# Multi-level linear attention stage: GpSimd in program order, expert-row gathers by quarters, narrow state sums, turned keys, and three small moves in the scan stage

## The chip, the cores and the metric

One core of one Trainium2 chip runs the whole program. The metric is the device time of one execution in microseconds, the median of three runs. The trace is of one further, profiled execution, which has a time of its own.

## What is computed

A stack of four layers, each an attention-like half and a feed-forward half behind an adaptive layer norm, works on 32 sequences of 256 tokens with 128 features. The change touches two halves. The first is the selective scan of layer 0:

```python
delta = softplus(delta @ dt_W.T + dt_b)             # and softplus of the two convolutions
h = exp(delta * A) * h + delta * u * B               # 16 states for each of 128 features, along 256 tokens
y = sum_n(h * C) + u * D                             # two branches, then x = x + ga * (y*z + h)
```

The second, which gives the change its name, is the attention of layer 1. For each of 16 heads of width 8 it adds a causal linear attention and four more of the same kind, whose keys and values are causal block means over 2, 4, 8 and 16 tokens (`L` levels), and mixes the sum with a local softmax attention over 64 tokens:

```python
phi = lambda t: elu(t) + 1
for each of two chunks of 128 tokens:
    out  = phi(q) @ s_kv + causal(phi(q) @ phi(k).T) @ v     # s_kv: sum of phi(k).T @ v of the chunk before
    norm = the same with v = 1
glob = sum over 5 sets of (out / norm) * weight
```

The input of this half is the output of the expert layer before it, which lies in DRAM, two rows (one for each chosen expert) for each token. They are gathered by row number and added with their weights.

## The kernel before

**Layout.** `x` is kept in 16 tiles `x[b]` of 128 features by 512 tokens (two sequences). The stages of `run` (L2741) follow one another; the scan is `scan_layer` (L637), the multi-level attention is `hale` (L1544).

**Who sets the order.** Work is written as an agenda: `put(t, f)` hangs a function on a step `t`, and the agenda is run through in order of `t`. That is the program order. Only instructions that go through `keep_in_program_order` are held to it: TensorE's always (L386, L390), ScalarE's where `strict_act` is set, and VectorE's where `nc.vector.on` is set (class `InOrder`, L288). All the others are placed by the toolchain's planner, which sends the earliest written of those that it believes ready to an idle engine. In the scan, TensorE and ScalarE are in program order, VectorE and GpSimd are planned. In `hale`, TensorE alone is in program order.

**The scan.** For each tile there are eight steps `p` (two branches of four groups of four states); a tile begins every 16 agenda steps, an even and an odd one for each `p`. `scan_even` (L828) has TensorE fill all four banks of `dB` (16 matmuls), VectorE run four scans `hs` (L847), and then issues `scan_weigh(p-2, 1)`, `scan_turned(p-1, 0)` and `scan_decay(p+1, 0)`; `scan_odd` (L852) issues the other halves. `scan_turned` (L865) transposes half of `hs` into `hT` (one buffer) and ScalarE copies it to `hsT`; `scan_weigh` (L877) sums `hsT` with `Cd` into `y`; `scan_decay` is two exponentials on ScalarE. Beside them each tile has its preparation: four times `soft_start` (L734; `Abs` on ScalarE and `max(x+b, 0)` on VectorE, both from the one PSUM buffer `tp`) and `soft_end` (L741; Exp, Ln, and an addition on GpSimd), `scan_rows` (L765), `scan_b`, `scan_c`; and its end, `scan_end` (L899): VectorE adds `y`, GpSimd multiplies by `z` and adds `h`, and `residual` (L525) on VectorE writes `x[b]`. Here k stands for p modulo 8; the end of a tile falls on the odd step of k = 1 of the next.

**The multi-level attention.** `hale_slots` (L1589) gives each of 32 sequences `q` sixteen steps from `T = 16q`. Steps T to T+5 are the local attention (`hale_window`, with the maxima `hale_max` of the next sequence beside it), steps T+6 to T+15 the five linear attentions in two chunks each: `hale_scores` (L1873) fills two `S` tiles (two buffers in all), one is masked by VectorE (L1888), the other is copied by ScalarE (L1890) and masked by GpSimd (L1891, `affine_select`), and one step later `hale_weighted` (L1895) multiplies both with the values. The rest is hung between: 

- `gather_rows` (L1234) at T-48 for even q (T = 32b): eight indirect DMAs from GpSimd's queue into `got` (one buffer), and `gather_add` (L1249) at T-38: `gather_sum` on VectorE (L1261, L1262), four transposes, `residual`.
- `hale_values` (L1807): values of one half, and for half 0 the keys of set 0 in rows (`w.vvk`), through `phi` (L1655: Exp and Relu on ScalarE, one VectorE instruction) into `kt[:, 0]`.
- `hale_level_values(a, 0, pair)` (L1818): keys and values of two levels for half 0, keys through `phi` into `kt`; `hale_level_values(a, 1, None)`: values of all four for half 1.
- `hale_features` (L1835) and `hale_level_keys` (L1850): keys in columns for the scores, through `phi` into `f`; and GpSimd's `qG` (L1843).
- `hale_states` (L1861): `kt` times the values of half 0, 256 columns for each of five sets, masked by VectorE into `kvs`.
- `hale_divide` (L1927) transposes, divides and lets GpSimd add into `glob` (L1957); `hale_gate` (L1959) mixes and writes the residual.

All of these share three PSUM buffers `tp`. Within a step, first the `main` matmuls are issued, then their ScalarE, VectorE and GpSimd parts, then `side`, then `last`:

```python
            if s == 0:
                if self.gather:
                    put(side, T - 48, lambda b=b: self.gather_rows(b))
                    put(side, T - 38, lambda b=b: self.gather_add(0, b))
...
            put(side, T - 3, lambda a=a: self.hale_level_values(a, 0, 0))
            put(side, T - 2, lambda a=a: self.hale_level_keys(a, 0))
            put(side, T - 2, lambda a=a: self.hale_states(a, (0, 1)))
            put(side, T + 0, lambda a=a: self.hale_level_keys(a, 1))
            put(side, T + 1, lambda a=a: self.hale_level_values(a, 0, 1))
            put(side, T + 2, lambda a=a: self.hale_level_values(a, 1, None))
            put(side, T + 3, lambda a=a: self.hale_states(a, (2, 3)))
            put(side, T + 4, lambda a=a: self.hale_states(a, (4,)))
```

Of the kernel before, what the change touches and what calls it, by code (L numbers as in the profile page):

```python
# [30 lines left out]
P = 128  # L31
# [144 lines left out]
def packs(d):  # L176
# [40 lines left out]
    k.add("WoT", g["Wo"].T)  # L217
    k.add("Wk", g["Wk"])
    k.add("Wv", g["Wv"])
    k.add("vvk", np.concatenate([g["Wv"].T, g["Wvl"].T, by_heads(g["Wk"].T, DENSE)], 1))  # L220
# [67 lines left out]
class InOrder:  # L288
# [4 lines left out]

    def __getattr__(self, name):
        op = getattr(self.engine, name)
        if not self.on:
            return op
        return lambda *args, **kw: self.tc.keep_in_program_order(op(*args, **kw))  # L298


class Engines:
    def __init__(self, tc):
        self.nc = tc.nc
        self.vector = InOrder(tc, tc.nc.vector)

    def __getattr__(self, name):
        return getattr(self.nc, name)
# [2 lines left out]
class Program:  # L310
# [326 lines left out]
    def scan_layer(self, w):  # L637
# [7 lines left out]
        with ExitStack() as ctx:  # L645
# [28 lines left out]
            for b in range(NB):  # L674
                a = s[b] = {"b": b}
                T = 16 * b
                put(T, self.clear_regions)

                for o, n, src in ((T - 40, 1, lambda a: self.x[a["b"]]), (T - 32, 2, lambda a: a["h"])):
                    put(o, lambda a, n=n, src=src: a.update({("st", n): self.norm_rows(src(a), self.nc.gpsimd)}), a)  # L680
                    put(o + 1, lambda a, n=n: self.scan_roots(a, n), a)
                    put(o + 3, lambda a, n=n: self.norm_scale(a["st", n][0], *a["r", n]), a)
                put(T - 36, self.scan_norm_out, a)
                put(T - 28, self.scan_norm_out2, s, a)
                put(T - 23, self.scan_proj, s, a)
# [12 lines left out]
                put(T + 19, self.scan_end, s, a)  # L698
            for t in sorted(agenda):
                for f, args in agenda[t]:  # L700
                    f(*args)
# [126 lines left out]
    def scan_even(self, s, p):  # L828

        nc = self.nc  # L830
        if 0 <= p < 8 * NB:
# [13 lines left out]
            for n in range(4):  # L845
                decay = s["decay"][(4 * p + n) % 10].rearrange("p s t -> p (s t)")
                nc.vector.tensor_tensor_scan(hs[:, :, n], decay, dB[:, :, n], 0.0, ALU.mult, ALU.add)  # L847
# [51 lines left out]
    def scan_end(self, s, a):  # L899
        nc = self.nc  # L900
        py = self.ps("tp", (P, 4, P))
        for i in range(4):
            self.tr(py[:, i, :], a["yT"][:, i, :])
        y = self.wk("y")
        cut = dict(i=4, r=32)
        nc.vector.tensor_tensor(
            y.rearrange("p (q i r) -> p q i r", **cut),
            a["uu"].rearrange("p (q i r) -> p q i r", **cut),
            py.rearrange("p i (q r) -> p q i r", q=4),
            ALU.add,  # L910
        )
        nc.gpsimd.tensor_tensor(y, y, a["z"], ALU.mult)
        nc.gpsimd.tensor_tensor(y, y, a["h"], ALU.add)
        self.residual(0, 0, a["b"], y)


    def clear_regions(self):
# [313 lines left out]
            j, n = a["j"], m["BLK"]  # L1231
            self.nc.sync.dma_start(m["eo"][j * n : (j + 1) * n, :].rearrange("(t p) f -> p t f", p=P), eo)

    def gather_rows(self, b):  # L1234

        got = self.wk("got", (P, 4, 2, P))
        for t in range(4):
            for k in (0, 1):
                self.nc.gpsimd.indirect_dma_start(
                    out=got[:, t, k, :],  # L1240
                    out_offset=None,
                    in_=self.gather["eo"][:, :],
                    in_offset=bass.IndirectOffsetOnAxis(ap=self.back[:, k, 4 * b + t : 4 * b + t + 1], axis=0),
                    bounds_check=self.gather["rows"] - 1,
                    oob_is_err=False,
                )
        self.gather[b] = got

    def gather_add(self, layer, b):  # L1249
        self.gather_sum(b, range(4))  # L1250
# [293 lines left out]
    def hale(self, w):  # L1544
        nc, c = self.nc, self.c
        BF = mybir.dt.bfloat16
        with ExitStack() as ctx:
# [38 lines left out]
            self.strict = False  # L1586
            self.gather = None

    def hale_slots(self, w):  # L1589
# [9 lines left out]
        for q in range(2 * NB):  # L1599
# [26 lines left out]
            put(side, T - 6, lambda a=a: self.hale_values(w, a, 0))  # L1626
            put(side, T - 5, lambda a=a: self.hale_values(w, a, 1))
            put(side, T - 4, lambda a=a: self.hale_features(w, a))
            put(side, T - 3, lambda a=a: self.hale_level_values(a, 0, 0))
            put(side, T - 2, lambda a=a: self.hale_level_keys(a, 0))  # L1630
            put(side, T - 2, lambda a=a: self.hale_states(a, (0, 1)))
            put(side, T + 0, lambda a=a: self.hale_level_keys(a, 1))
            put(side, T + 1, lambda a=a: self.hale_level_values(a, 0, 1))
            put(side, T + 2, lambda a=a: self.hale_level_values(a, 1, None))
            put(side, T + 3, lambda a=a: self.hale_states(a, (2, 3)))
            put(side, T + 4, lambda a=a: self.hale_states(a, (4,)))
            for n in range(5):
                for i in (0, 1):
                    t = T + 6 + 2 * n + i
# [8 lines left out]
        for t in range(min(side), max(side) + 1):  # L1648
            then = [work() for work in main.get(t, [])]
            for work in then:  # L1650
                work()
# [154 lines left out]

    def hale_values(self, w, a, t):  # L1807

        n = 3 if t == 0 else 2
        pv = self.ps("tp", (P, n, P))  # L1810
        self.mm(pv, a["h"][:, t * P : (t + 1) * P], w.vvk[:, 0 : n * P])
        self.nc.vector.tensor_copy(
            self.vzb[t][:, :, :, 0:8], pv[:, 0:2, :].rearrange("p n (h d) -> p n h d", d=8)
        )
        if t == 0:
            self.phi(self.kt[:, 0, :], pv[:, 2, :])

    def hale_level_values(self, a, t, pair):  # L1818

        if t == 0:  # L1820
            pv = self.ps("tp", (P, 2, 2, P))
            for l in (0, 1):
                lvl = 2 * pair + l
                self.mm(pv[:, l], a["hm"][:, lvl, 0:P], self.wl[:, lvl])
            lv = slice(2 * pair, 2 * pair + 2)
            src = pv[:, :, 1, :]
            self.phi(self.kt[:, 1 + 2 * pair : 3 + 2 * pair, :], pv[:, :, 0, :])
        else:
            src = self.ps("tp", (P, 4, P))
            for lvl in range(4):  # L1830
                self.mm(src[:, lvl, :], a["hm"][:, lvl, P:], self.wl[:, lvl, 1, :])
            lv = slice(0, 4)
        self.nc.vector.tensor_copy(self.vzl[t][:, lv, :, 0:8], src.rearrange("p l (h d) -> p l h d", d=8))

    def hale_features(self, w, a):  # L1835

# [23 lines left out]

    def hale_states(self, a, ns):  # L1861

        pk = self.ps("tp", (P, len(ns), SEQ))
        for m, n in enumerate(ns):
            self.mm(pk[:, m, :], self.kt[:, n, :], self.set_values(n, 0)[:, :, 0:16])
        self.nc.vector.tensor_tensor(
            self.kvs[:, ns[0] : ns[-1] + 1, :],
            pk,
            self.c.same.unsqueeze(1).to_broadcast([P, len(ns), SEQ]),
            ALU.mult,  # L1870
        )

# [928 lines left out]
```

## Time and profile before

| What | Value |
|---|---|
| median of three runs | 6856.3 us (6840.84 to 6861.61) |
| the profiled execution | 6756.19 us, its span 6754.3 us, mean granted clock of TensorE 0.934 |
| scan stage, first to last scan instruction | 125.0 us to 1144.3 us |
| `hale`, first TensorE instruction to the next stage | 1717.9 us to about 3840 us |
| one tile in the scan (eight steps), in the middle | 64.8 us |
| two sequences (one tile) in `hale`, in the middle | 130.4 us |

A line of the groups reads: source line, engine, operation, what is written from what, shapes, count, busy time and mean of one, then the idle time of the engine just before them and what ended it. A line of the waits reads: who waited, on whom, total time, how often, the longest. A line of the timeline reads: start, duration, engine, line, operation, and in brackets the idle time before it and what ended that. PEld is TensorE's weight load; POOL is GpSimd, DVE VectorE, ACT ScalarE. The trace counts a float32 matmul as two instructions.

### The profile page before, as it was taken

To read this page: it belongs to the slowest core of one execution; us is meant where nothing else is said; L and a number is where in the kernel's file an instruction comes from. 1 tells how busy PE (TensorE), PEld (TensorE's weight loads), DVE (VectorE), ACT (ScalarE), POOL (GpSimd) and SP (SyncE) were. 2 spreads that over 40 slices of the span, in tenths; PEclk is the share of its full clock that TensorE was granted. 3 is DMA by queue.
4 is the path that set the end of the run, shared out by engine and by line. 5 is a ranking of instruction groups with operands and counts; after the bars stand their busy time and mean duration, and the time that the engine had idled before them with its cause. 6 is when DMAs were issued, how large, how long until landed. Compare 5 with 4: busy or idle time off the path is not lost. (4 is left out here: it accounts for less than half of the span.)

```text
span 6754.3 us, 132930 instructions
## 1 busy us (share of the span) xinstructions
PE 5907.4 (87%) x54209; PEld 3313.6 (49%) x54209; DVE 4350.0 (64%) x10025; ACT 3557.5 (53%) x5227; POOL 2660.5 (39%) x2881
## 2 busy tenths in 40 slices
PE   5777776899899999999999887999889998999987
PEld 3555555457555555555566444454422222444444
DVE  3666766621466666666666572888677774777779
ACT  5888885233344444444445442444478886544532
POOL 3555553566444444444444362444244543000000
PEclk7999998899899999999999877999999998989988
DMA  1101101135100000000000101111133442000010
GB/s 60 41 28 41 41 29 36 41 109 134 28 7 5 5 5 8 5 5 8 5 2 2 45 4 38 25 27 28 31 84 90 92 91 48 15 18 18 18 33 30
DMA packets 175447, 232.27 MB, mean 34 GB/s; under 512 B 46519, under 2 KB 95919, under 8 KB 174450
## 3 DMA queue, kind: packets, MB, share of 16 engines
q1 hardware_dynamic: 120656, 124.47, 7.3%
q0 software_dynamic: 26992, 56.62, 3.6%
q10 hardware_dynamic: 27186, 42.67, 1.7%
q8 instruction: 426, 6.98, 0.4%
q14 instruction: 187, 1.53, 0.1%
HBM read 88.28 MB, written 74.97 MB: 24 GB/s over the span
## 5 line engine op out<-in xcount | busy, mean ns | idle before, releaser
L1416 ACT ACTIVATE E<-S 128x1024 f32<-128x1024 f32 x448 | 459.0, 1025 | 592.8 <-PE S L386 579.4
L847 DVE TENSOR_TENSOR_SCAN hs<-decay,dB 128x512 f32<-128x512 f32 x512 | 583.1, 1203 | 196.9 <-PE dB L386 114.7
L298 DVE TENSOR_REDUCE mt<-S 128x4 f32<-128x1024 f32 (+1 forms) x512 | 550.2, 1088 | 224.5 <-PE S L386 223.8
L386 PE MATMUL S<-qa,kx 32*128 32x256 f32 x4096 | 556.2, 392 | 59.6 <-DVE mt L298 59.1
L393 ACT ACTIVATE hid<-S,bigw 128x1024 f32<-128x1024 f32 x512 | 537.6, 1112 | 124.2 <-PE S L386 124.0
L1888 DVE TENSOR_TENSOR E<-S,cst 128x1024 f32<-128x1024 f32 x320 | 391.2, 1223 | 301.1 <-PE S L386 300.5
L1891 POOL TENSOR_SCALAR_AFFINE_SELECT E<-E 128x1024 f32<-128x1024 f32 x320 | 350.2, 1094 | 594.6 <-ACT E L1890 594.2
L386 PE MATMUL S<-kx,q 32*128 32x512 f32 (+1 forms) x2048 | 540.4, 623 | 17.1 <-ACT kx L1534 16.1
L1890 ACT COPY E<-S 128x1024 f32<-128x1024 f32 x320 | 323.7, 1012 | 315.1 <-PE S L386 315.1
L2440 POOL TENSOR_TENSOR acc<-acc,ye 128x512 f32<-128x512 f32 x256 | 344.7, 1347 | 360.4 <-DVE ye L298 318.1
L386 PEld LDWEIGHTS S<-qa,kx 32*128 32x128 f32 x4096 | 350.8, 195 | 174.6 <-DVE mt L298 137.1
L1713 DVE TENSOR_REDUCE mt<-S 128x4 f32<-128x512 f32 (+1 forms) x256 | 205.2, 823 | 294.0 <-PE S L386 293.8
L386 PE MATMUL S<-qG,f 32*128 32x512 f32 x2560 | 382.3, 657 | 7.5 <-DVE E L1888 6.4
L386 PE MATMUL S<-hm,bigw 32*128 32x512 f32 x2048 | 338.7, 654 | 25.2 <-ACT hid L393 25.2
L393 ACT ACTIVATE hsT<-hT 128x1024 f32<-128x1024 f32 x256 | 260.4, 1017 | 179.7 <-PE hT L390 179.4
L390 PE MATMUL hT<-cst,hs 128*128 128x128 f32 x2048 | 285.9, 283 | 75.4 <-ACT hsT L393 73.5
L393 ACT ACTIVATE decay<-dl,A 128x510 f32<-128x510 f32 x512 | 339.2, 714 | 0.0
L386 PE MATMUL po<-E,vzl 128*32 128x128 f32 x8192 | 284.1, 279 | 50.1 <-POOL E L1891 50.1
L1760 ACT ACTIVATE E<-S 128x768 f32<-128x768 f32 (+1 forms) x192 | 169.1, 881 | 280.7 <-PE S L386 279.9
L390 PEld LDWEIGHTS hT<-cst,hs 128*128 128x128 f32 x2048 | 225.1, 143 | 169.6 <-ACT hsT L393 139.7
L386 PE MATMUL po<-E,vz 128*32 128x256 f32 x4096 | 300.2, 379 | 7.2 <-POOL E L1420 6.9
L386 PE MATMUL po<-hid,bigw 128*32 128x512 f32 x2048 | 277.2, 613 | 30.4 <-DVE ye L298 30.4
(520 smaller groups left out, 13307.8 us busy)
## 6 DMA issues: line engine op xcount, KB each, us to landing
gb<-gT SPq DMA_DIRECT2D x256, 256.0 KB
regions<-zeros ACTq DMA_DIRECT2D x16, 2048.0 KB
rx<-far SPq DMA_DIRECT2D x64, 256.0 KB
expert_rows<-eo SPq DMA_DIRECT2D x39, 256.0 KB
out<-out SPq DMA_DIRECT2D x16, 256.0 KB
xTd<-xT SPq DMA_DIRECT2D x15, 256.0 KB
xT<-xTd SPq DMA_DIRECT2D x15, 256.0 KB
bigw<-in_s SPq DMA_DIRECT2D x10, 256.0 KB
```

What stands on the lines that cost most here:

```text
L298: return lambda *args, **kw: self.tc.keep_in_program_order(op(*args, **kw))
L386: return self.tc.keep_in_program_order(self.nc.tensor.matmul(out, lhsT, rhs, start=start, stop=stop, **kw))
L390: return self.tc.keep_in_program_order(self.nc.tensor.transpose(out, in_, self.c.ident[:k, :k]))
L393: ins = self.nc.scalar.activation(*args, **kw)
L847: nc.vector.tensor_tensor_scan(hs[:, :, n], decay, dB[:, :, n], 0.0, ALU.mult, ALU.add)
L1416: nc.scalar.activation(e, src, AF.Exp, scale=scale)
L1713: nc.vector.tensor_reduce(m.rearrange("p (g j) -> p g j", j=2), pm[:, :, x] if i == 0 else pm[:, :, :, 0:192], AX.X, ALU.max, negate=True,)
L1760: nc.scalar.activation(e, src, AF.Exp, scale=1.0 / math.sqrt(8))
L1888: nc.vector.tensor_tensor(e, src, self.c.caus.unsqueeze(1).to_broadcast([P, 8, P]), ALU.mult)
L1890: nc.scalar.copy(e, src)
L1891: nc.gpsimd.affine_select(e, e, [[0, 8], [1, P]], ALU.is_ge, 0.0, base=0, channel_multiplier=-1)
L2440: nc.gpsimd.tensor_tensor(a["acc"], a["acc"], ye, ALU.add)
```

## The change

In the scan: `soft_start` no longer uses ScalarE's `Abs`; VectorE makes `m = src - 2 r` from `r = max(src + bias, 0)`, and `soft_end` takes `exp(m + bias)`. The residual of a tile is written two steps later in the agenda. `scan_even` issues `scan_weigh` after `scan_turned` and `scan_decay`.

In `hale`: GpSimd is held to program order (its DMAs are not, but each gather now reads its row numbers from `own`, a small copy that is). A tile's gather is split into four quarters of two DMAs, at T-62, T-58, T-54 and T-50, the sums at T-52 to T-40, the transposes and the residual stay at T-38. The row-wise keys of half 0 are no longer multiplied out: `hale_turn_keys` transposes the column-wise ones. The state sums take nine columns of each head in place of sixteen, and `kvs` is zeroed once.

```diff
 class InOrder:
-        if not self.on:
+        if not self.on or "dma" in name:
             return op
 class Engines:
         self.vector = InOrder(tc, tc.nc.vector)
+        self.gpsimd = InOrder(tc, tc.nc.gpsimd)
...
                 put(T + 19, self.scan_end, s, a)
+                put(T + 21, lambda a: self.residual(0, 0, a["b"], a["y"]), a)
     def soft_start(self, src, bias):
         m, r = self.wk("sp_m"), self.wk("sp_r")
-        self.act(m, src, AF.Abs, bias=bias)
         self.nc.vector.tensor_scalar(r, src, bias, 0.0, ALU.add, ALU.max)
-        return m, r
-    def soft_end(self, out, m, r):
-        self.act(m, m, AF.Exp, scale=-1.0)
+        self.nc.vector.scalar_tensor_tensor(m, r, -2.0, src, ALU.mult, ALU.add)
+        return m, r, bias
+    def soft_end(self, out, m, r, bias):
+        self.act(m, m, AF.Exp, bias=bias)
     def scan_even(self, s, p):
-        self.scan_weigh(s, p - 2, 1)
         self.scan_turned(s, p - 1, 0)
         self.scan_decay(s, p + 1, 0)
+        self.scan_weigh(s, p - 2, 1)
     def scan_end(self, s, a):
-        self.residual(0, 0, a["b"], y)
-    def gather_rows(self, b):
+    def gather_rows(self, b, quarters=range(4)):
+        got = self.gather[b]
+        for t in quarters:
+            at = [self.back[:, k, 4 * b + t : 4 * b + t + 1] for k in (0, 1)]
+            if nc.gpsimd.on:
+                own = self.wk("own", (P, 2), I32)
+                nc.gpsimd.tensor_copy(own, self.back[:, :, 4 * b + t])
+                at = own[:, 0:1], own[:, 1:2]
             for k in (0, 1):
...
     def hale(self, w):
+            nc.gpsimd.memset(self.kvs, 0.0)
-            self.strict = True
+            self.strict = nc.gpsimd.on = True
     def hale_slots(self, w):
-                    put(side, T - 48, lambda b=b: self.gather_rows(b))
-                    put(side, T - 38, lambda b=b: self.gather_add(0, b))
+                    for t in range(4):
+                        put(last, T - 62 + 4 * t, lambda b=b, t=t: self.gather_rows(b, (t,)))
+                        put(side, T - 52 + 4 * t, lambda b=b, t=t: self.gather_sum(b, (t,)))
+                    put(side, T - 38, lambda b=b: self.gather_end(0, b))
-            put(side, T - 3, lambda a=a: self.hale_level_values(a, 0, 0))
-            put(side, T - 2, lambda a=a: self.hale_level_keys(a, 0))
-            put(side, T - 2, lambda a=a: self.hale_states(a, (0, 1)))
-            put(side, T + 0, lambda a=a: self.hale_level_keys(a, 1))
-            put(side, T + 1, lambda a=a: self.hale_level_values(a, 0, 1))
-            put(side, T + 2, lambda a=a: self.hale_level_values(a, 1, None))
-            put(side, T + 3, lambda a=a: self.hale_states(a, (2, 3)))
-            put(side, T + 4, lambda a=a: self.hale_states(a, (4,)))
+            put(side, T - 3, lambda a=a: self.hale_level_keys(a, 0))
+            put(side, T - 2, lambda a=a: self.hale_level_keys(a, 1))
+            put(side, T + 0, lambda a=a: self.hale_level_values(a, 0))
+            put(side, T + 1, lambda a=a: self.hale_turn_keys(a, (0, 1, 2)))
+            put(side, T + 2, lambda a=a: self.hale_level_values(a, 1))
+            put(side, T + 3, lambda a=a: self.hale_turn_keys(a, (3, 4)))
+            put(side, T + 4, lambda a=a: self.hale_states(a, (0, 1, 2)))
+            put(side, T + 5, lambda a=a: self.hale_states(a, (3, 4)))
     def hale_values(self, w, a, t):
-        n = 3 if t == 0 else 2
-        pv = self.ps("tp", (P, n, P))
-        self.mm(pv, a["h"][:, t * P : (t + 1) * P], w.vvk[:, 0 : n * P])
+        pv = self.ps("tp", (P, 2, P))
+        self.mm(pv, a["h"][:, t * P : (t + 1) * P], w.vv)
...
-        if t == 0:
-            self.phi(self.kt[:, 0, :], pv[:, 2, :])
+    def hale_level_values(self, a, t):
+        pv = self.ps("tp", (P, 4, P))
+        for lvl in range(4):
+            self.mm(pv[:, lvl, :], a["hm"][:, lvl, t * P : (t + 1) * P], self.wl[:, lvl, 1, :])
+        self.nc.vector.tensor_copy(self.vzl[t][:, :, :, 0:8], pv.rearrange("p l (h d) -> p l h d", d=8))
+    def hale_turn_keys(self, a, ns):
+        pk = self.ps("tp", (P, len(ns), P))
+        for m, n in enumerate(ns):
+            self.tr(pk[:, m, :], a["f"][:, 1 + n, 0:P])
+        self.nc.scalar.copy(self.kt[:, ns[0] : ns[-1] + 1, :], pk)
     def hale_states(self, a, ns):
-        pk = self.ps("tp", (P, len(ns), SEQ))
+        pk = self.ps("tp", (P, len(ns), 16, 9))
         for m, n in enumerate(ns):
-            self.mm(pk[:, m, :], self.kt[:, n, :], self.set_values(n, 0)[:, :, 0:16])
+            self.mm(pk[:, m], self.kt[:, n, :], self.set_values(n, 0)[:, :, 0:9])
+        same = self.c.same.rearrange("p (h d) -> p h d", d=16)[:, :, 0:9]
         self.nc.vector.tensor_tensor(
-            self.kvs[:, ns[0] : ns[-1] + 1, :],
+            self.kvs[:, ns[0] : ns[-1] + 1, :].rearrange("p n (h d) -> p n h d", d=16)[:, :, :, 0:9],
...
```

More of the change, by code (lines that the diff above doesn't have):

```diff
@@ L219, in packs @@
     k.add("Wv", g["Wv"])
-    k.add("vvk", np.concatenate([g["Wv"].T, g["Wvl"].T, by_heads(g["Wk"].T, DENSE)], 1))
+    k.add("vv", np.concatenate([g["Wv"].T, g["Wvl"].T], 1))
     k.add("haar_Wk", np.stack([by_heads(diag_blocks(g["haar_Wk"][lvl].T, 16), DENSE) for lvl in range(4)], 1))
@@ L903, in scan_end @@
             self.tr(py[:, i, :], a["yT"][:, i, :])
-        y = self.wk("y")
+        y = a["y"] = self.wk("y")
         cut = dict(i=4, r=32)
@@ L1232, in block_out @@
             self.nc.sync.dma_start(m["eo"][j * n : (j + 1) * n, :].rearrange("(t p) f -> p t f", p=P), eo)
-    def gather_rows(self, b):
-        got = self.wk("got", (P, 4, 2, P))
-        for t in range(4):
+    def gather_rows(self, b, quarters=range(4)):
+        nc = self.nc
+        if 0 in quarters:
+            self.gather[b] = self.wk("got", (P, 4, 2, P))
+        got = self.gather[b]
[5 more added lines that the diff above has]
+                at = own[:, 0:1], own[:, 1:2]
             for k in (0, 1):
-                self.nc.gpsimd.indirect_dma_start(
+                nc.gpsimd.indirect_dma_start(
                     out=got[:, t, k, :],
@@ L1242, in gather_rows @@
                     in_=self.gather["eo"][:, :],
-                    in_offset=bass.IndirectOffsetOnAxis(ap=self.back[:, k, 4 * b + t : 4 * b + t + 1], axis=0),
+                    in_offset=bass.IndirectOffsetOnAxis(ap=at[k], axis=0),
                     bounds_check=self.gather["rows"] - 1,
@@ L1246, in gather_rows @@
                 )
-        self.gather[b] = got
     def gather_add(self, layer, b):
@@ L1582, in hale @@
             nc.vector.tensor_scalar(sw, sw, mx, None, ALU.mult)
-            self.strict = True
+            self.strict = nc.gpsimd.on = True
             self.use_ln_exp()
             self.hale_slots(w)
-            self.strict = False
+            self.strict = nc.gpsimd.on = False
             self.gather = None
@@ L1647, in hale_slots @@
                 put(side, T + 20 + 2 * n, lambda a=a, n=n: self.hale_gate(w, a, n))
-        for t in range(min(side), max(side) + 1):
+        for t in range(min([*side, *last]), max(side) + 1):
             then = [work() for work in main.get(t, [])]
@@ L1807, in hale_values @@
     def hale_values(self, w, a, t):
-        n = 3 if t == 0 else 2
-        pv = self.ps("tp", (P, n, P))
-        self.mm(pv, a["h"][:, t * P : (t + 1) * P], w.vvk[:, 0 : n * P])
-        self.nc.vector.tensor_copy(
-            self.vzb[t][:, :, :, 0:8], pv[:, 0:2, :].rearrange("p n (h d) -> p n h d", d=8)
-        )
-        if t == 0:
-            self.phi(self.kt[:, 0, :], pv[:, 2, :])
[L1818 to L1833, printed above, removed]
+        pv = self.ps("tp", (P, 2, P))
+        self.mm(pv, a["h"][:, t * P : (t + 1) * P], w.vv)
+        self.nc.vector.tensor_copy(self.vzb[t][:, :, :, 0:8], pv.rearrange("p n (h d) -> p n h d", d=8))
+    def hale_level_values(self, a, t):
[8 more added lines that the diff above has]
+        self.nc.scalar.copy(self.kt[:, ns[0] : ns[-1] + 1, :], pk)
     def hale_features(self, w, a):
@@ L1861, in hale_states @@
     def hale_states(self, a, ns):
-        pk = self.ps("tp", (P, len(ns), SEQ))
+        pk = self.ps("tp", (P, len(ns), 16, 9))
         for m, n in enumerate(ns):
-            self.mm(pk[:, m, :], self.kt[:, n, :], self.set_values(n, 0)[:, :, 0:16])
+            self.mm(pk[:, m], self.kt[:, n, :], self.set_values(n, 0)[:, :, 0:9])
+        same = self.c.same.rearrange("p (h d) -> p h d", d=16)[:, :, 0:9]
         self.nc.vector.tensor_tensor(
-            self.kvs[:, ns[0] : ns[-1] + 1, :],
+            self.kvs[:, ns[0] : ns[-1] + 1, :].rearrange("p n (h d) -> p n h d", d=16)[:, :, :, 0:9],
             pk,
-            self.c.same.unsqueeze(1).to_broadcast([P, len(ns), SEQ]),
+            same.unsqueeze(1).to_broadcast([P, len(ns), 16, 9]),
             ALU.mult,
```

## The prediction

> **What bounds the kernel now.** I read the busy times by stretch first, then who waited in each stage, then the timelines of the few microseconds in which the waits fall. The columns of the first are: stretch, length, then busy time of PE, PEld, DVE, ACT, POOL, granted clock.
>
> ```profile
> 2141.00:2272.00 131.00, 124.44 (x1392) 75.79 (x1392) 81.67 (x161) 61.47 (x103) 58.96 (x63) 0.99 0.02 6
> 3512.00:3636.00 124.00, 121.88 (x1394) 75.07 (x1394) 79.11 (x150) 61.16 (x102) 50.40 (x55) 1.00 0.01 2
> 600.80:665.60 64.80, 49.78 (x702) 34.56 (x698) 44.84 (x56) 53.45 (x89) 35.73 (x43) 0.97 0.10 36
> ```
>
> The first two are one tile of `hale` each, with a gather in it and (near the end, where none is left) without. TensorE is busy 95% and 98%; no other engine passes 65%. So `hale` runs at TensorE's pace, and what TensorE does or waits for there is the time. The tile with a gather takes 6.5 us more (the mask copies `vzb` of one sequence recur after 61.07 + 69.35 = 130.42 us in the middle, after 61.07 + 62.84 = 123.91 us at the end). The third stretch is a tile of the scan: nobody is full. The waits of `hale` name the reason for the 6.5 us:
>
> ```profile
> PE po L386 <- POOL E L1891: 50.1, 12, 4.2
> POOL got L1239 <- DVE gy L1262: 44.2, 14, 3.3
> ```
>
> Twelve waits of 4.2 us, one for each of tiles 4 to 15. POOL's timeline and PE's at one of them:
>
> ```profile
> 2145.43 1.03 POOL L1239 DMA_INDIRECT got<-expert_rows,back  x1 [3.30 <-DVE gy L1262]
> ...
> 2152.44 1.00 POOL L1239 DMA_INDIRECT got<-expert_rows,back  x1 [0.30 <-issue]
> 2153.45 1.11 POOL L1891 TENSOR_SCALAR_AFFINE_SELECT E<-E 128x1024 f32<-128x1024 f32 x1
> ```
>
> ```profile
> 2149.79 0.65 PE L386 MATMUL po<-E,vzl 128*32 128x128 f32 x16
> 2154.61 0.89 PE L386 MATMUL po<-E,vzl 128*32 128x128 f32 x16 [4.18 <-POOL E L1891]
> 2155.43 2.09 PE L386 MATMUL S<-qG,f 32*128 32x512 f32 x8
> ```
>
> The planner let the next tile's gather follow the sums that free `got`, some 22 steps ahead of where it is written; POOL's queue then stands 3.30 us for VectorE and issues six DMAs at 1.3 us apart, while a mask whose input was there at 2145.9 (end of the ScalarE copy) waits until 2153.45. After the stall the next score group takes 2.09 us where the same one took 1.14 before.
>
> In the scan the least step is 5.9 us: four scans (4.55), then the sixteen `dB` matmuls (1.17), since `dB` has one buffer; the last steps show 5.90. The eight steps of a tile take 7.48, 6.63, 8.12, 8.89, 6.99, 7.68, 12.22 and 6.82 us (k = 3 to 2). The 12.22 is this:
>
> ```profile
> DVE x L533 <- POOL y L913: 65.1, 14, 4.7
> ```
>
> ```profile
> 651.94 0.69 DVE L906 TENSOR_TENSOR y<-uu,tp 128x512 f32<-128x512 f32 x1 [0.77 <-PE tp L390]
> 657.35 1.52 DVE L533 SCALAR_TENSOR_TENSOR x<-y,mods,x 128x256 f32<-128x256 f32 x2 [4.72 <-POOL y L913]
> 658.79 4.54 DVE L847 TENSOR_TENSOR_SCAN hs<-decay,dB 128x512 f32<-128x512 f32 x4
> ```
>
> VectorE stands 4.72 us for the residual with the next `dB` complete since 653.0.
>
> **What the Trainium skill says.** "TensorE: Matmul & The Clock Gate", Part 1, has the array fall to half clock after an idle window of about 3.4 us and need about as long of work to come back; the 1.14 that became 2.09 us behind 4.18 us of idling agrees. "GPSIMD Engine Reference", section 4, has GpSimd's own cores write the descriptors of its DMAs, so that they hold its queue; 1.0 us each and 0.3 between agrees. "Perfetto Trace Analysis", section "DMA Instruction — SWDGE (GPSIMD)", ends the profiled interval with the last descriptor and not with the data: the trace gives 2.5 to 4.8 us (median 3.1) from issue to landing.
>
> **Gathers by quarters, GpSimd in order.** A quarter is a copy of 128x2 (nearest row: 0.20 us for 128x4, L481) and two DMAs, 2.6 us, at steps 2, 6, 10, 14 of even q behind that step's mask. The `got` buffer was freed ten steps before, so the 3.30 us go. What queues behind the pair is the next step's mask: at steps 6 and 10 its input comes later than the DMAs end; at 2 and 14, where a `glob` addition (0.73) stands before, it starts up to 2.8 us late. It was read 3.4 us after its input and 1.1 us of work in the case above, so it is just covered. I take the stall as gone. It is worth the difference of the pairs less the four transposes that stay (0.49): 130.42 - 123.91 - 0.49 = 6.0 us (4.18 of waiting, 0.95 + 0.39 + 0.24 of slow groups behind it, the rest small): 12 x 6.0 = **-72 us**. Otherwise POOL's order is what it was: masks, `glob`, `qG` already stand in program order.
>
> The sums (0.24 + 0.31 us a quarter) are planned on VectorE as soon as the planner believes the rows landed. Unlike before, when they lay in `got` for 100 us, VectorE may now reach them early. Queued behind are the mask L1888 and the maxima, which free `S`: mask ended 2091.1, next score group began 2091.88, so 0.75 us is free. The wait is between nothing and all of 2.6 + 3.1 = 5.7 us; 14 tiles come in steady state, 56 quarters, so 0 to 56 x 4.95 = 277 us. I take **+10**: a step is 3.8 us and a landing ends inside the next one, where some VectorE work stands before it.
>
> **Narrow sums and turned keys.** On TensorE, by the timeline, a sequence: values of half 0 go from 384 to 256 columns, 0.85 to 0.63 (-0.21); level values from 2 x 0.87 to the 0.98 that half 1 takes (-0.76); states from 0.86 + 0.97 + 0.53 = 2.36 to five of 144 columns, which I price like 128 (0.245 each, from 0.98 for four) with two starts of 0.1, 1.43 (-0.93; nothing if the weight load or the nine-of-32 pattern costs as much as before); transposes in groups of three and two, 0.38 + 0.31 (from 0.44 for four, 0.31 for two) = +0.69. Sum -1.2 us, between -0.3 and -1.5; times 32 = **-39 us**. Off the path: ScalarE loses 0.55 + 4 x 0.38 of `phi` and gains two copies (0.48, 0.38); VectorE loses 2.4 us of `phi` and about 0.8 of masks. `hale_level_keys` moves three and two steps forward past other `tp` work; each brings 1.06 us of matmuls, 1.2 of ScalarE, 0.7 of VectorE, as at its old place. States move to T+4 and T+5, three steps ahead of their first reader at T+8. All of that has slack at the present 65% and 50%.
>
> **Start of hale.** `kvs` zeroing adds 1280 elements, 1.15 us (1.81 for 2048, L1558), ahead of the first gather, on which TensorE waits (13.17 us); four copies and their waits add up to 2: **+3 us**.
>
> **Scan.** Four `Abs` of 0.68 us leave ScalarE, four VectorE instructions join; the nearest are 0.69 (L906, one operand in PSUM) and 1.33 (L727, none): I take 0.72. The bank `tp` is then free 5.87 us after a step's scans begin (4.47 + 0.66 + 0.74); it was 5.68, 5.84 and 5.20 at k = 3, 5, 7, and TensorE needs it ahead of the next `dB`: +0.2, 0, +0.7. Against it, k = 6 waits for a chain through ScalarE (`sp_m`, then POOL's `dl`, `du`, `Xr`), which comes 0.4 to 0.7 earlier, and with `hT` filled ahead of `scan_weigh`'s 0.64 us ScalarE starts `hsT` 0.35 to 0.6 earlier at k = 4 and 1. Walking the eight steps, the chain that ends the 12.22 (ScalarE's `sp_m`, POOL's `dl`, `y*z`, `du`, `y+h`) comes 0.6 us earlier a tile, between -1.2 and +0.8: 15 x -0.6 = **-9 us**.
>
> The residual's move: I take nothing for it. VectorE is planned here, and the planner hoists what it believes ready (in `hale` it put the sums of a later tile at 2143.23, right behind a residual that is written after them by a whole tile's steps). It had placed the residual ahead of scans whose `dB` was complete 4.3 us before `y`, so it must have believed `y` ready before `dB`; written two steps later it is still that.
>
> **Sum.** -72 + 10 - 39 + 3 - 9 = -107 us on the profiled 6756.2 (span 6754.3 and 1.9 around it): 6649. The median of the runs shown, 6856.3, is 1.015 times the profiled one; I scale alike: -108, **6748 us**, own range 6715 to 6785.
>
> **Rivals.** (A) The residual does move behind the scans. For it: its written place is then after them. The step at k = 1 becomes 12.22 - 4.7 and ScalarE, busy 53 of 65 us, can follow: 15 x -5 = -75, 76 scaled: 6672. Chance 0.17. (B) Slower: VectorE's wait for the landings takes the place of POOL's stall. From a loss of 117/56 = 2.1 us of TensorE a quarter (2.85 us of VectorE waiting less 0.75) the gain is gone; at 4 us of waiting, 56 x 3.25 = 182 - 117 = +65: 6921. For it: the fixed 3.1 us and the hoisting; against it: the `got` waits on VectorE total 7.1 us now and lie at the start. Chance 0.10. (C) The pair of DMAs at steps 2 and 14 still makes masks late, or the landings cost 1 us a quarter: half the gain is left, 6800. Chance 0.14. (D) The parts cancel within the bound: 0.04. My forecast has 0.55.
>
> **Numbers.** The measurement can tell about 0.3% (20 us) from no change. Faster: the forecast, A and C, 0.86; same 0.04; slower 0.10. The range goes from A's time with room below it to C's with room above: 6655 to 6810.
>
> **What would show it.** Right: no `po` wait on `E` L1891 of about 4 us, tile periods in `hale` near 122 us with and without a gather, the gather's DMAs in pairs; `tp<-vzl,kt` near 0.25 us a matmul. In the scan: periods near 64 us, with VectorE still standing over 4 us for POOL's `y`; if that is gone, A. Wrong: waits of VectorE's `gy` on the landing of `got` above 2 us each with TensorE idle behind the mask L1888 (B).

## The result, and the profile after

The change made the kernel slower: 6901.0 us (median of four runs, 6893.2 to 6904.7) against 6851.4, a ratio of 1.0065 with a 95% interval from 1.0051 to 1.0080. A second set of runs gave 1.0069 (1.0052 to 1.0085). That is some 50 us more where 108 us less was predicted.

The profiled execution after has a span of 6896.9 us, 142.6 us more than the one before, which is more than the 50 us. The rest doesn't belong to the change. The kernel before took 6758 us in one set of runs (experiment 1) and 6851 to 6871 in the other three, and the difference lies in stages that the change doesn't touch. The stretch from the last scan to the first `dk` transpose took 262 us in the profile before and 282 us after, but also 296 us in a kernel with only the scan edits that ran beside the second set. So the kernels below are compared by their ratio to the kernel before, run beside them, and by the lengths of stages that repeat to 0.3%. In those terms the change cost 43.7 us in the multi-level attention (from `identb` to `zero`, 2120.9 to 2164.6 us) and between -4 and +3 us in the scan.

The busy times by stretch, in the kernel after: a tile with a gather, one sequence near the end without (the pair's first half), and a tile of the scan (columns as in the prediction):

```profile
2566.00:2699.00 133.00, 124.32 (x1399) 77.84 (x1398) 76.69 (x148) 59.33 (x95) 58.81 (x66) 0.95 0.02 5
3506.00:3564.00 58.00, 56.55 (x659) 35.57 (x655) 37.81 (x80) 29.00 (x48) 29.11 (x33) 1.00 0.02 6
...
600.00:664.80 64.80, 51.83 (x698) 36.40 (x698) 46.69 (x61) 51.91 (x86) 35.68 (x43) 0.92 0.10 36
```

The tile with a gather grew from 131 to 133 us and TensorE's granted clock in it fell from 0.99 to 0.95; without a gather the clock is still 1.00. So the loss belongs to the gathers. The waits of that stage (who waited on whom: us in total, times, longest):

```profile
DVE gy L1270 <- DMA got<-expert_rows,own: 107.8, 42, 4.9
PE S L387 <- DVE E L1894: 95.9, 45, 4.4
...
DVE gy L1271 <- DMA got<-expert_rows,own: 29.9, 29, 2.3
```

TensorE's twelve waits of 4.2 us on GpSimd's mask are no longer there: that stall was removed, as meant. Two others have come. VectorE stands 137.7 us (107.8 + 29.9) for gathered rows to land, and TensorE 95.9 us for VectorE's mask. Before, the second of these waits was:

```profile
PE S L386 <- DVE E L1888: 13.1, 44, 1.0
```

Where they meet, on VectorE, GpSimd and TensorE, at the fourth quarter of one tile:

```profile
2647.69 0.68 DVE L1675 SCALAR_TENSOR_TENSOR f<-phi_e,phi_r 128x512 f32<-128x512 f32 x1
2652.03 0.91 DVE L1270 TENSOR_SCALAR gy<-got,pair 128x128 f32<-128x128 f32 x1 [3.66 <-DMA got<-expert_rows,own]
2652.86 1.21 DVE L1894 TENSOR_TENSOR E<-S,cst 128x1024 f32<-128x1024 f32 x1
```

```profile
2647.86 1.10 POOL L298 TENSOR_TENSOR glob<-glob,lv 128x256 f32<-128x256 f32 x1 [0.65 <-DVE lv L1952]
2648.91 0.18 POOL L298 COPY own<-back 128x2 int32<-128x2 int32 x1
2649.36 1.05 POOL L1249 DMA_INDIRECT got<-expert_rows,own  x1 [0.27 <-POOL own L298]
2650.72 1.01 POOL L1249 DMA_INDIRECT got<-expert_rows,own  x1 [0.31 <-issue]
```

```profile
2647.72 1.14 PE L387 MATMUL S<-qG,f 32*128 32x512 f32 x8
2648.80 1.08 PE L387 MATMUL po<-E,vzl 128*32 128x128 f32 x32
2654.12 1.65 PE L387 MATMUL S<-qa,k 32*128 32x192 f32 x8 [4.25 <-DVE E L1894]
2655.70 1.03 PE L387 MATMUL S<-loc0b,identb 128*128 128x512 bf16 x2
2656.67 2.08 PE L387 MATMUL S<-k,qs 32*128 32x256 f32 x8
```

Read from VectorE's second line. It has had nothing to do since 2648.4, and the scores that its mask needs are complete at 2648.9; but the sum of the quarter stands ahead of the mask in its queue, and its rows come only at 2652.0. The sum is written ten steps (38 us) behind its DMAs; here VectorE was given it a microsecond before GpSimd had even issued them (2649.36). The mask frees the `S` buffer at 2654.1, and TensorE, whose last work ended at 2649.9, stood all that time. Then it works slowly: the three groups take 1.65, 1.03 and 2.08 us. One sequence earlier they took 0.92, 0.61 and 1.13:

```profile
2585.38 0.92 PE L387 MATMUL S<-qa,k 32*128 32x192 f32 x8 [0.30 <-DVE E L1894]
2586.23 0.61 PE L387 MATMUL S<-loc0b,identb 128*128 128x512 bf16 x2
2586.77 1.13 PE L387 MATMUL S<-k,qs 32*128 32x256 f32 x8
```

The stretches behind the waits show why (eighth figure: the granted clock):

```profile
2634.50:2636.50 2.00, 1.99 (x10) 0.96 (x11) 1.20 (x3) 0.54 (x1) 0.00 (x0) 0.71 0.00 0
2636.50:2638.50 2.00, 2.00 (x9) 1.62 (x8) 1.16 (x4) 0.95 (x2) 1.09 (x1) 0.50 0.00 0
...
2654.10:2656.50 2.40, 2.38 (x10) 1.28 (x10) 0.23 (x1) 0.68 (x1) 0.00 (x0) 0.50 0.00 0
2656.50:2658.50 2.00, 2.00 (x9) 1.18 (x8) 0.00 (x0) 0.13 (x1) 1.27 (x2) 0.50 0.04 8
```

The pairs in the middle have two such places each, at the third and the fourth quarter: TensorE waits 2.06 us and 4.25 us (at two of twelve third quarters longer than 2.06). Behind the first the groups to the next `po<-f,kvs` take 4.55 us where they took 2.91 one sequence earlier, behind the second those to the next `S<-qa,k` 9.32 us against 5.39 (5.83 less a transpose of 0.44 that only the earlier one has). Sum: 2.06 + 1.64 + 4.25 + 3.93 = 11.9 us. A pair without these waits is 59.57 + 61.90 = 121.5 us in this trace; one with them is 133.1 in the middle and 133.4 on average, so 11.6 to 11.9 us are to be explained, and the sum does it.

That the slow groups are the clock's doing shows in two tiles, at 2103 and 2236 us, where the same wait of 2.06 us left the clock at 1.00. There the same groups took 2.91 us, as one sequence earlier:

```profile
2103.30 1.14 PE L387 MATMUL S<-qG,f 32*128 32x512 f32 x8 [2.06 <-DVE E L1894]
...
2106.21 0.61 PE L387 MATMUL po<-f,kvs 128*128 128x128 f32 x4
```

```profile
2103.30:2105.30 2.00, 2.00 (x14) 1.14 (x15) 1.36 (x3) 0.71 (x1) 0.00 (x0) 1.00 0.00 0
```

The pairs of these two tiles still take 132.8 and 133.0 us; where the rest of their time goes was not followed.

### The profile page after: what moved, and what is told of

It is laid out like the page before. It is cut to its first block, busy times and chain, and to the rows that moved or that the text cites. A ratio compares the mean times of both kernels' runs of the same rounds, so it can differ in the third digit from the quotient of the medians.

```text
span 6896.9 us, 132934 instructions
## 1 busy us (share of the span) xinstructions
PE 5986.9 (87%) x54369; PEld 3398.6 (49%) x54369; DVE 4301.0 (62%) x9929; ACT 3502.3 (51%) x5035; POOL 2674.1 (39%) x2946
## 5 line engine op out<-in xcount | busy, mean ns | idle before, releaser
L298 POOL TENSOR_SCALAR_AFFINE_SELECT E<-E 128x1024 f32<-128x1024 f32 (+1 forms) x704 | 631.4, 897 | 880.6 <-ACT E L1896 586.2
L1894 DVE TENSOR_TENSOR E<-S,cst 128x1024 f32<-128x1024 f32 x320 | 391.0, 1222 | 240.2 <-PE S L387 238.7
L1726 DVE TENSOR_REDUCE mt<-S 128x4 f32<-128x512 f32 (+1 forms) x256 | 205.0, 822 | 304.6 <-PE S L387 304.5
L391 PE MATMUL hT<-cst,hs 128*128 128x128 f32 x2048 | 305.3, 297 | 38.5 <-ACT hsT L394 37.2
L391 PEld LDWEIGHTS hT<-cst,hs 128*128 128x128 f32 x2048 | 245.1, 151 | 111.0 <-ACT hsT L394 88.1
L1429 POOL TENSOR_SCALAR_AFFINE_SELECT E<-E 128x512 f32<-128x512 f32 (+1 forms) x192 | 158.2, 825 | 362.3 <-ACT E L1425 362.0
```

Of the source, the lines that this page charges most:

```text
L391: return self.tc.keep_in_program_order(self.nc.tensor.transpose(out, in_, self.c.ident[:k, :k]))
L1429: nc.gpsimd.affine_select(part, part, [[0, n], [1, P]], ALU.is_ge, 0.0, base=0, channel_multiplier=-1)
L1726: nc.vector.tensor_reduce(m.rearrange("p (g j) -> p g j", j=2), pm[:, :, x] if i == 0 else pm[:, :, :, 0:192], AX.X, ALU.max, negate=True,)
L1894: nc.vector.tensor_tensor(e, src, self.c.caus.unsqueeze(1).to_broadcast([P, 8, P]), ALU.mult)
```

## Experiments

The theory after this reading, called "landing" in the expectations: VectorE's wait for gathered rows, with a ready mask queued behind it, costs the gain of everything else. Its rivals: GpSimd's program order makes its own masks late ("GpSimd's order"), and the keys and states at their new steps crowd the shared buffers ("crowding").

**1. The kernel before, once more.**

> The kernel before, profiled once more. Its first profiled execution is 95 us under the median of its timed ones (6756 against 6851), and three stretches that the change does not touch are shorter in it than in the profile after: 1154 to 1406 us 250 against 271, 3841 to 4065 us 223 against 260, 4178 to 4850 us 671 against 722. Theory 'by chance': this difference lies in that one execution; the new profile has stretches near 271, 260 and 722 and about 6850 us in all, with the same 130.4 us per pair of sequences in the multi-level attention. Rival 'the change reaches them': the stretches are again 250, 223 and 671.

Measured: 6759.0 us, against 6758.1 of the other runs of the kernel before in this set (ratio 1.0004, 0.9995 to 1.0012); 130.7 us a pair; the stretches nearly as in the first profile (262 us from the last scan to the first `dk` transpose, 224, and 682 where it was 671). This fits neither wording as a whole: the stretches are those that the rival named, but the timed runs of the same kernel are now as fast as its profile. So the profile before was no chance execution; the first timed runs, 6851 us, came under other conditions. The record has this set on another chip than the two later ones, and at another hour; which of the two it is, the runs don't tell. Experiment 5 decides whether the change has to do with it.

**2. The sums behind copies of their weights.**

```diff
     def gather_sum(self, b, quarters):
...
-            at = slice(4 * b + t, 4 * b + t + 1)
+            at = self.pair[:, :, 4 * b + t]
+            if nc.gpsimd.on:
+                at = self.wk("ownp", (P, 2))
+                nc.gpsimd.tensor_copy(at, self.pair[:, :, 4 * b + t])
-            nc.vector.tensor_scalar(y[:, t, :], got[:, t, 0, :], self.pair[:, 0, at], None, ALU.mult)
+            nc.vector.tensor_scalar(y[:, t, :], got[:, t, 0, :], at[:, 0:1], None, ALU.mult)
...
```

> The kernel after with one edit: the sums of a gathered quarter take their weights from a copy of 128x2 that GpSimd makes in program order at the step where the sums are written, so VectorE can't be given them earlier. Theory 'landing' (VectorE stands for the rows with a ready mask behind it): a pair with a gather falls from 133.1 us to 120 to 122 (a pair without one takes 119.4), the waits of gy on got go to nearly nothing, 14 x 11 to 13 us = 155 to 185 less than 6901, so 6715 to 6745. Rival 'GpSimd's order' (its masks come late behind the DMAs and glob): pairs stay above 130, time within 20 us of 6901. Rival 'crowding' (turned keys and states at their new steps): the same, above 130.

Measured: 6698.9 us, ratio 0.9917 (0.9903 to 0.9930); a pair takes 125.3 us, not 120 to 122. Against the kernel after (1.0069) that is 1.5% less, some 103 us, so the sums' place is most of the loss and both rivals are out as its main cause. But not all came back. The waits of this kernel name the rest:

```profile
DVE gy L1273 <- POOL ownp L298: 62.0, 43, 2.6
...
PE S L387 <- DVE E L1897: 49.2, 50, 2.9
```

VectorE now stands for the copy instead of the rows: the planner again put the sum into its queue ahead of what the sum needs.

**3. Gathers and GpSimd's order alone**, on the kernel before: only the hunks of `InOrder`, `gather_rows`, the `put` of quarters and sums, and the switch `nc.gpsimd.on`.

> The kernel before with GpSimd in program order and the gathers by quarters alone; keys, states and scan as before. Theory 'landing': a pair is 123.9 + 13.2 = 137 us against 130.4, so 14 x 6.6 = +92 us: about 6940. Rival 'crowding': without the turned keys the gathers give what was forecast, -60 us: about 6790. 'GpSimd's order' expects the first as well, but with masks of GpSimd late instead of waits for got.

Measured: 6825.5 us, ratio 1.0110 (1.0093 to 1.0127), +67 us; a pair takes 134.8 us. That is less than the +92 us and the 137 us of the theory, but on its side. Keys and states are as before, and the waits come with the gathers all the same:

```profile
PE S L387 <- DVE E L1900: 95.0, 45, 4.6
...
DVE gy L1270 <- DMA got<-expert_rows,own: 77.5, 36, 4.0
```

**4. Narrow sums and turned keys alone**, on the kernel before.

> The kernel before with narrow state sums and turned keys alone. Theory 'landing': this part only gains, 16 pairs by 2.4 us (forecast of the sum) to 4.5 us (pairs without a gather, 123.9 to 119.4): 6780 to 6815. Rival 'crowding': within 10 us of 6851 or above it.

Measured: 6744.5 us, ratio 0.9981 (0.9972 to 0.9990): -14 us, less than forecast. The stage got 17 us shorter. A pair without a stall takes 121.45 us against 123.90, the forecast's 2.4 us less; a pair with a gather, in the middle, only 129.7 against 130.7. What is missing went into the old stall, which got longer (12 times 4.2 us before):

```profile
PE po L386 <- POOL E L1885: 65.8, 12, 5.5
```

TensorE came sooner to a mask that GpSimd finishes no sooner. A part that gains by itself, and its full size where nothing stalls, leaves nothing for the rival of crowding.

**5. The kernel after, once more.**

> The kernel after, once more, because the kernel before takes 6758 us in these runs and took 6851 beside the first runs of the kernel after. Theory 'the chip': the unchanged stretches are now 250, 223 and 671 us as in every profile of these runs, the multi-level attention is as slow as before (even sequences near 71 us), and the time is about 6758 + 50 = 6808. Rival 'the change reaches the other stages': 271, 260 and 722 us again.

Measured: 6917.4 us beside 6871.2 of the kernel before, 1.0069 (1.0052 to 1.0085). Neither wording holds: the time is not near 6808 us, but the kernel before is also near 6870 us in this set. In the multi-level attention the profile repeats the first one to a microsecond or two (even sequences 71.13 us, the stage 2163.0 us). The three stretches are 288 (from the last scan), 256 and 733 us, close to the rival's, yet in experiment 7, with unchanged code there, they are 296, 265 and 730. They go with the set of runs, not with the change.

**6. Masks, maxima and sums in program order on VectorE.**

```diff
+            held, nc.vector.on = nc.vector.on, nc.vector.on or nc.gpsimd.on
             nc.vector.tensor_scalar(y[:, t, :], got[:, t, 0, :], self.pair[:, 0, at], None, ALU.mult)
...
+            nc.vector.on = held
```

and the same switch around the maxima (L1726) and the mask (L1894).

> The kernel after with VectorE's masks, maxima and the sums of the gathered quarters (and nothing else on VectorE) held in program order, so that the sums stand ten steps, some 38 us, behind their DMAs; no copies of the weights. Theory 'landing': no waits on got or on copies, even sequences fall from 71.2 to about 60, the pair to 121 or 122: 50 us less than the kernel whose sums wait for copies of their weights (6699), so about 6650. Rival 'GpSimd's order': what was left there (125.3 us a pair) is its masks behind its DMAs, and it stays: 6690 to 6710.

Measured: 6795.3 us, ratio 0.9891 (0.9872 to 0.9911), 1.8% or 122 us under the kernel after. No wait of VectorE on `got` or on a copy is left in the stage, and TensorE keeps its full clock through a tile with a gather:

```profile
2500.00:2624.40 124.40, 118.86 (x1406) 73.99 (x1404) 77.47 (x148) 59.38 (x94) 59.19 (x66) 1.00 0.02 6
```

The pair is 124.4 us, not 121 to 122. Its sequences without a gather take 60.3 and 60.5 us against 59.6 and 59.8, so about half of the 3 us comes with the held order itself and half with the gather. TensorE's wait for VectorE's masks is shorter each time and more frequent:

```profile
PE S L387 <- DVE E L298: 58.4, 80, 2.4
```

**7. The scan edits alone**, on the kernel before.

> The kernel before with the three edits of the scan stage alone. Forecast's walk: 0.6 us less a tile, 6758 - 9 = 6749. The trace after gives a tile of 64.76 against 64.78 us: 6754. Rival: VectorE is the dearer place for the work that left ScalarE and a tile gets longer (65.4 in the kernel with the held sums): 6768.

Measured: 6871.9 us, ratio 1.0004 (0.9992 to 1.0016). Nothing that can be told from zero: the interval runs from -5 to +11 us, and the forecast's -9 us lies just outside it.

**8. The same, with the residual held behind the scans.**

```diff
+                self.tc.keep_in_program_order(
                     nc.vector.tensor_tensor_scan(hs[:, :, n], decay, dB[:, :, n], 0.0, ALU.mult, ALU.add)
+                )
...
+            if self.strict_act and (layer, half) == (0, 0):
+                self.tc.keep_in_program_order(ins)
```

> As the scan edits alone, with VectorE's scans and this residual held in program order to each other, so that the residual really comes behind the scans of the step. Theory 'the planner kept it in place' (the residual's VectorE stall of 4.7 us a tile is on the path, and the move as written doesn't take effect): the step k = 1 falls from 11.9 to about 7.2 us, 15 x 4.7 = 70 us less than without it: about 6680. Rival: the chain through ScalarE and GpSimd ends no earlier and the wait goes elsewhere: within 15 us of the scan edits alone.

Measured: 6800.7 us, ratio 0.9893 (0.9873 to 0.9914): 71 us less than the scan edits alone. The step k = 1 takes 5.99 us in place of 11.86, a tile 60.1 in place of 64.6.

**9. Both orders held** (6 and 8 together, on the kernel after).

> The kernel after with both orders held: masks, maxima and gathered sums in the multi-level attention, scans and the residual in the scan stage. The two gains lie in stages that follow one another and should multiply: 0.9891 x (0.9893 / 1.0004) = 0.978 of the time before, some 150 us less. Rival: one eats the other (a denser scan lowers the granted clock of the next stage): 0.983 to 0.989.

Measured: 6730.4 us, ratio 0.9789 (0.9769 to 0.9809). The two gains multiply. The change as written, in two orders that it didn't hold, is 2.1% faster than the kernel before.

**10. As 9, the maxima planned again.**

> As the kernel with both orders held, but VectorE's maxima are planned again; only masks and gathered sums are held. With the maxima held, a sequence without a gather took 60.3 to 60.5 us against 59.6 to 59.8 in the kernel after. If the held maxima cost that, 32 x 0.7 = 22 us less; if the order of the masks costs it, the same time.

Measured: 6725.5 us, ratio 0.9796 (0.9777 to 0.9815), and sequences without a gather at 60.3 and 60.5 us as in 6 and 9. The held maxima cost nothing; the masks in program order do, or the sums among them. Which of the two was not separated.

**11. As 6, with GpSimd planned.** Only the switch for GpSimd is left out; the copies of row numbers and the quarters stay.

> As the kernel after with masks, maxima and sums held on VectorE, but GpSimd planned and not in program order (the gathers still by quarters behind copies of their row numbers). Theory 'landing': GpSimd's order is not what costs or gains, the sums' place is: 0.989 of before and a pair near 124.4 us again. Rival: without its order the planner bunches the DMAs ahead of a mask as in the kernel before: a pair at 128 to 131, 0.994 to 0.999.

Measured: 6902.6 us, ratio 1.0049 (1.0032 to 1.0066), a pair at 131.8 us, slower still than the rival's 128 to 131 us and 0.994 to 0.999. Its mechanism is there: without its program order GpSimd is again handed DMAs too early and stands in its queue for the sums that free `got`, as in the kernel before (44.2 us there):

```profile
POOL got L1250 <- DVE gy L298: 40.7, 14, 19.9
```

How that reaches TensorE was not followed: its own waits on GpSimd's masks sum to only 11.6 us in this trace. But the switch is all that differs from experiment 6, so GpSimd's order is no burden; it is one of two orders that the quarters need.

**12. The residual alone, moved and held**, on the kernel before, without the other two scan edits.

> The kernel before with the residual of the scan written two steps later and held behind the scans, without the other two scan edits. If the residual's place is the whole gain, the same as with them: 0.989. If ScalarE's four Abs and the order of scan_weigh become the bound once the stall is gone (ScalarE then has 53 of 60 us), it is 1 to 2 us a tile worse: 0.991 to 0.994.

Measured: 6787.3 us, ratio 0.9882 (0.9865 to 0.9900), a tile of 59.8 us: as good as with the other edits. VectorE at the end of a tile, first in the kernel after, then in this one:

```profile
656.65 0.69 DVE L908 TENSOR_TENSOR y<-uu,tp 128x512 f32<-128x512 f32 x1 [0.24 <-PE tp L391]
662.27 1.52 DVE L534 SCALAR_TENSOR_TENSOR x<-y,mods,x 128x256 f32<-128x256 f32 x2 [4.93 <-POOL y L915]
663.72 2.32 DVE L849 TENSOR_TENSOR_SCAN hs<-decay,dB 128x512 f32<-128x512 f32 x2
```

```profile
616.19 0.69 DVE L911 TENSOR_TENSOR y<-uu,tp 128x512 f32<-128x512 f32 x1 [0.78 <-PE tp L390]
617.39 4.57 DVE L851 TENSOR_TENSOR_SCAN hs<-decay,dB 128x512 f32<-128x512 f32 x4 [0.52 <-PE dB L386]
621.86 1.29 DVE L533 SCALAR_TENSOR_TENSOR x<-y,mods,x 128x256 f32<-128x256 f32 x2
```

In the first, VectorE stands 4.93 us for GpSimd's `y` with the scans behind it. In the second, four scans fill just that time.

## Why the prediction was wrong

**The step that failed** is the price of the sums' wait: "I take **+10**: a step is 3.8 us and a landing ends inside the next one, where some VectorE work stands before it." It was 11.9 us a tile, 14 x 11.9 = 167 us, within the bounds of 0 to 277 that the same paragraph had worked out. Two things in it were wrong.

- Where the sum would stand. The prediction said that VectorE "may now reach them early", and then took a place a step behind the DMAs. The planner put the sum into the step of the DMAs themselves, in the case above 1.0 us ahead of their issue. The kernel before held the evidence. The sums that start at 2143 us there are transposed only at 2272 us, and the rows whose DMAs start at 2145 us only at 2402 us. With 4.08 us a step (130.4 / 32), and the gather written ten steps ahead of its transposes, the sums stood some 32 steps ahead of their place and the gather some 53, not the 22 of the prediction. So no distance in the agenda was a cover.
- What a wait costs. VectorE's waits were counted at their own length less 0.75 us of slack. The slow groups behind a TensorE stall were counted for the stall that goes (4.18 us of waiting made 6.0), not for the one that comes. They are 1.64 + 3.93 = 5.6 of the 11.9 us.

**Rival B was right in mechanism, and nearly in its time**: 6921 with a chance of 0.10, against 6901. The time is in part luck: B took 4 us of waiting at each of four quarters and nothing behind it, where VectorE waited 2.5 us on average and TensorE lost its time at two quarters, almost half of it in slow groups. The `got` waits counted against B, 7.1 us, were those of one of the two sums; both had 18.2 us, though at the start as it says. Its break-even was set by the same faulty price: 2.85 us of VectorE waiting a quarter. VectorE stood 137.7 / 56 = 2.5 us a quarter, below it, and the gain was gone all the same, since TensorE lost 167 / 56 = 3.0 us a quarter where 2.1 were to be the limit.

**GpSimd's stall**: right. The 4.2 us waits are gone. In the kernel before, a pair with a gather took 130.7 us against 123.9, so 6.8 x 12 = 82 us came back; 72 were forecast. (The 82 and the 167 both contain the four transposes of a tile, 0.49 us, which stay.)

**Narrow sums and turned keys**: right to the size. -1.2 us a sequence were forecast; pairs without a stall went from 123.90 to 121.47, -1.21 a sequence. The states' five groups take 0.85 + 0.62 = 1.47 us by their starts, 1.43 forecast. Taken alone it showed as 14 us in place of 39, because the stall that it runs into grew (experiment 4).

**Start of hale**: +3 forecast; from `identb` to the first `vzb` copy 49.9 us became 52.7.

**Sum of the stage**: -82 + 167 - 39 + 3 = +49, measured +43.7.

**Scan**: -9 forecast, nothing that can be told from zero measured (1.0004, 0.9992 to 1.0016). By the medians of the steps, the walk was right where it saw a gain at k = 4 (6.6 to 6.0 us) and k = 1 (12.2 to 11.9), and in the price of the longer hold of `tp` at k = 3 (7.5 to 7.8) and k = 7 (7.0 to 7.8). It was wrong at k = 6, where it had a chain come 0.4 to 0.7 us earlier and the step grew instead (8.9 to 9.3); why was not tested. The tile stays at 64.8 us.

**The residual's move**: right that it takes no effect as written. The kernel after has the wait still, 15 times 4.8 us:

```profile
DVE x L534 <- POOL y L915: 71.9, 15, 5.0
```

Rival A was right on its worth: -75 us forecast, 71 us measured once the order is held (8 against 7). The cause given for the planner's choice, that it believes `y` ready before `dB`, was argued and not tested.

**The scale** of 1.015 from the profile to the median was taken as a property of the kernel. It belonged to the set of runs: in experiment 1 the profiled execution takes 6760.9 us and the median 6759.0.

## What to carry to other kernels

Where a planner places the instructions, holding the queue that issues a transfer can be half a measure, as it was here: its reader was placed ahead of the landing, and its wait held what stood behind it (a mask with its input there at 2648.9 us began at 2652.9). Hold the reader and its neighbours too (1.0069 became 0.9891), and look in the trace after for the wait on the other side of each buffer. Price a new stall as you price the one that goes, with the slow work behind it; and where a step that is moved in the source shows the same wait at the same place, the move hasn't taken place: held, this one was worth 1.1%.

## What the runs showed of the hardware

TensorE's clock can fall after shorter waits than I had thought, and the length of the wait alone does not decide it. "TensorE: Matmul & The Clock Gate", Part 1, speaks of an idle window of about 3.4 us. In the kernel after, ten tiles from 1969 to 3437 us have a wait of just 2.06 us at the third quarter: in the four microseconds behind it the mean granted clock is 0.57 to 0.63 in eight of them and 1.00 in two. At 2634.5 us, where work began again, the clock stood at 1.00 for another 0.9 us, then at 0.50 until 2638.75. In experiment 6 a wait of 2.05 us, ended at 3229.5 us, left it at 1.00, while two waits of 0.63 and 0.95 us, the second ended at 2020.6 us, were followed by 0.54 and then 0.50; the same two at 2523.2 us were not. What decides between them, no run here shows.
